# A graph message-passing layer: destination checks moved into the loop over edges, and the order of the last groups changed

## The chip, the cores and the metric

The kernel runs on one core of a Trainium2 chip. A core has a matrix engine (TensorE, PE in the profile; its weight loads are shown apart as PEld), a vector engine (VectorE, DVE), a scalar engine (ScalarE, ACT), GpSimd (POOL) and a sync engine (SP). Each runs its own list of instructions in order and waits on semaphores for the others. DMAs are started by SP, ACT and POOL. The metric is the device time of one execution in microseconds (us); lower is better.

## The reference, cut to what matters

There are N = 6250 nodes of H = 128 features and E = 100000 edges with 4 attributes each. The edges come sorted by destination.

```python
src, dst = edge_index
msg_in = concatenate([x[src], x[dst], edge_features], axis=1)      # E x 260
h = silu(msg_in @ mW1 + mb1)
messages = h @ mW2 + mb2
aggregated = segment_sum(messages, dst, num_segments=N)
u = silu(concatenate([x, aggregated], axis=1) @ uW1 + ub1)
updated = u @ uW2 + ub2
y = layer_norm(x + updated, ln_g, ln_b)
out = layernorm(x + y)                                             # no gain, no bias
```

All is float32.

## The kernel before

**Tables.** msg_in @ mW1 is split by rows of mW1. A table A = x @ mW1[:128] (`tab_a`) and a table B = x @ mW1[128:256] + mb1 (`tab_b`) are made once and stored to DRAM. For an edge, A is gathered by source; B is taken by destination.

**Groups.** The edges are worked on in 98 groups (NG) of 8 tiles of 128 edges (G = 8; the last group, 97, has 6 tiles). Because the edges are sorted, the destinations of one group lie within W = 96 neighbouring nodes from the group's first destination (`base`) on. For a group g:

- `fetch` (L267): POOL starts one indirect DMA per tile, which gathers 128 rows of A into a buffer `ga`. There are six such buffers, so group g+6 waits until group g's buffer has been read. `fetch(g + 4)` is called in iteration g. The first four groups (RAW) gather rows of x instead of A.
- `load` (L536): SP loads 96 rows of B from row `base` on (`mv`) and the edge attributes. The row number is in a register: every 14 groups `load_bases` (L525) reads 14 node numbers from `base_i` into registers of SP and DVE (a TENSOR_LOAD).
- `node_matrix` (L545, DVE) makes a 0/1 matrix `st` of nodes by edges; `edge_matrix` (L557, DVE) a 0/1 matrix `oh` of edges by nodes.
- `products` (L568, PE) adds B's rows and the attributes for each edge into PSUM (`pre`).
- `hidden` (L579): DVE adds gathered A and `pre` into `s` (L587), which frees the gather buffer, and ACT applies silu (L588, `h`). `s` is missing for the first four groups, where PE adds A itself.
- `by_nodes` (L591, PE) sums h over the edges of a node (`pt`, L597), after a transpose of the degree counts (L594). `add` (L600, DVE) adds the sums into the accumulator `acc`, the counts into `deg`.

In iteration g the order is: hidden(g), products(g+2), node_matrix(g+3), edge_matrix(g+1), add(g-2), by_nodes(g). PE, DVE, ACT and SP keep exactly the order in which the Python code calls them (a manual schedule, L111); POOL's only work in the loop is the gathers.

**Nodes.** When all edges of a batch of nodes are done, `node_batch` (L416) does the update for it: two accumulating matmuls and a third for the bias (L455 to L457, `y`), silu (L460, `uT`), a bias row and one matmul per tile (L462, L471), the residual (L473), two layer norms (L473 to L500) and the store (L504). It is a generator: each `yield` ends a step, and the loop runs one step of every running batch per iteration (two in the last six). Batches have 4 tiles of 128 nodes, the last two have 2; the one before the last starts in iteration 96, the last one (`final`) after the loop.

**Start.** Before the loop, POOL gathers for groups 0 to 3, PE transposes x, tables A and then B are made. In between `destination_lists` (L215) makes `rel` (the destination of each edge relative to its group's base), `base_i`, and then a check: the largest and smallest `rel` (L236, L237), 13 memsets (L250) and a few small operations give `bad_i`, which is 1 if some group spans more than 96 nodes or a batch would start too early. At the end every engine reads `bad_i` (L678) and branches to a general path that this data does not take. `fuse_weights` (L405) is called in iteration 5.

The numbers of the lines in this section are those of the kernel before.

Of the kernel before, what the change touches and what calls it, by code (L numbers as in the profile page):

```python
# [24 lines left out]
def kernel(  # L25
# [116 lines left out]
    def by_lane_now(g):  # L142

        t = consts.tile([P, G], I32, name=f"src{g}")
        nc.sync.dma_start(t, src[g * GE : (g + 1) * GE].rearrange("(i p) -> p i", p=P))
        return t

    src_0 = by_lane_now(0)
# [44 lines left out]
    src_i = consts.tile([P, NG, G], I32, name="src_i")  # L193
    rel = consts.tile([P, NG, G], F32, name="rel")
    base_p = consts.tile([P, NG], F32, name="base_p")
    base_i = consts.tile([1, NG], I32, name="base_i")
    bad_i = consts.tile([1, 1], I32, name="bad_i")

# [16 lines left out]
    def destination_lists():  # L215
        base_c = work.tile([NG, 1], F32, name="base_c", bufs=1)
        nc.vector.tensor_copy(base_c, dst_l[:, 0:1])
        rel_n = work.tile([P, GE], F32, name="s")[:NG]
        nc.vector.tensor_scalar(rel_n, dst_l, base_c, None, op0=OP.subtract)

        near_n = work.tile([P, GE], F32, name="s")[:NG]
        nc.vector.tensor_scalar(near_n, rel_n, float(W), -1.0, op0=OP.min, op1=OP.max)
        near_u = tpool.tile([NG, GE], U8, name="near_u")
        nc.vector.tensor_scalar(near_u, near_n, 1.0, None, op0=OP.add)
        nc.sync.dma_start(near_d[:, :], near_u)
        by_lane(rel, rel_n)
        base_f = work.tile([1, NG], F32, name="base_f", bufs=1)
        row = to_row(base_c, NG)
        nc.vector.tensor_copy(base_f, row)
        nc.vector.tensor_copy(base_i, row)  # L230
        p_b = narrow()
        nc.tensor.matmul(p_b[:, :NG], ones[0:1, :], base_f, start=True, stop=True)
        nc.vector.tensor_scalar(base_p, p_b[:, :NG], p_col, None, op0=OP.add)

        far = work.tile([NG, 2], F32, name="far", bufs=1)
        nc.vector.tensor_reduce(far[:, 0:1], rel_n, AX.X, OP.max)  # L236
        nc.vector.tensor_reduce(far[:, 1:2], rel_n, AX.X, OP.min)  # L237
        mid = (W - 1) / 2
        nc.vector.tensor_scalar(far, far, -mid, None, op0=OP.add)
        nc.vector.tensor_mul(far, far, far)  # L240
        nc.vector.tensor_reduce(far[:, 0:1], far, AX.X, OP.max)
        farthest = work.tile([1, 1], F32, name="farthest", bufs=1)
        nc.vector.tensor_reduce(farthest, to_row(far[:, 0:1], NG), AX.X, OP.max)
        bad = work.tile([1, 2], F32, name="bad", bufs=1)
        nc.vector.tensor_scalar(bad[:, 0:1], farthest, mid * mid, None, op0=OP.is_gt)

        below = work.tile([1, NG], F32, name="below", bufs=1)
        nc.vector.memset(below, 0.0)
        for i0, n, g in batches[:-1]:
            nc.vector.memset(below[:, g:], float((i0 + n) * P))  # L250
        nc.vector.tensor_sub(below, below, base_f)
        nc.vector.tensor_reduce(bad[:, 1:2], below, AX.X, OP.max)
        nc.vector.scalar_tensor_tensor(
            bad_i, bad[:, 1:2], 0.0, bad[:, 0:1], op0=OP.is_gt, op1=OP.max
        )
# [66 lines left out]
    def turn_x(i0, n):  # L322
# [2 lines left out]
            nc.tensor.transpose(pt[:, i, :], x_sb[:, i0 + i, :], ident)  # L325
        nc.scalar.copy(xT[:, i0 * P : (i0 + n) * P], pt[:, :n, :].rearrange("p i f -> p (i f)"))

    parts = groups(NT, G)

    def table(i0, n, half):  # L330
# [26 lines left out]
    destination_lists()  # L357
    attribute_rows(0)
    destinations(0)
    for k, (i0, n) in enumerate(parts):  # L360
        if k < RAW:
            turn_rows(k)

        tb = x_sb[:, i0 : i0 + n, :]
        nc.vector.tensor_add(tb, table(i0, n, 1), b1[:, None, :].to_broadcast([P, n, H]))
        nc.sync.dma_start(by_node(tab_b)[:, i0 : i0 + n, :], tb)
# [49 lines left out]
    def node_batch(i0, n, work, new, y, final=False):  # L416
# [30 lines left out]
        if not final:  # L447
# [3 lines left out]
            nc.scalar.copy(flat(deg_b), counts)  # L451
            sums, counts = flat(acc_b), flat(deg_b)
        yield
        y = y()
        nc.tensor.matmul(flat(y), u1x, xT[:, cols], start=True, stop=False)  # L455
        nc.tensor.matmul(flat(y), w2u, sums, start=False, stop=False)  # L456
# [15 lines left out]
        yield  # L472
        nc.vector.tensor_add(y[:, :n], y[:, :n], xs[:, :n])  # L473
        mv = moments(y)
        nc.vector.tensor_add(xs[:, :n], xs[:, :n], b_b[:, None, :].to_broadcast([P, n, H]))
        yield
        r = std(mv)
        yield
# [2 lines left out]
        for i in range(n):  # L481
            nc.vector.scalar_tensor_tensor(  # L482
                y[:, i, :], y[:, i, :], mv[:, i, 0:1], g_b, op0=OP.subtract, op1=OP.mult
            )
            nc.vector.scalar_tensor_tensor(  # L485
                z[:, i, :], y[:, i, :], r[:, i : i + 1], xs[:, i, :], op0=OP.mult, op1=OP.add
            )
        mz = moments(z)
        yield
# [11 lines left out]
                o[:, i, :], z[:, i, :], AF.Identity, bias=shift[:, i : i + 1], scale=rz[:, i : i + 1]  # L501
            )
        yield
        nc.sync.dma_start(rows_of(out), o[:m, :n])  # L504

    def node_tiles(pool, y):
        return pool, lambda name, p=P: pool.tile([p, BT, H], F32, name=name), y
# [14 lines left out]
    nodes = edges.enter_context(tc.tile_pool(name="nodes", bufs=1))  # L522
    stbuf = [held.tile([K1, GE], F32, name=f"st{k}") for k in range(NST)]

    def load_bases(g):  # L525
        _, vals = nc.values_load_multi_w_load_instructions(
            base_i[0:1, g : g + RB],
            engines=(ENG.SP, ENG.DVE),
            min_val=0,
            max_val=NP,  # L530
            skip_runtime_bounds_check_because=IN_RANGE,
        )
        for k, v in enumerate(vals):
            bases[g + k] = v

    def load(g):  # L536

        if g % NQ == 0 and g:
            destinations(g)
        if g % RB == 0:  # L540
            load_bases(g)
        nc.sync.dma_start(mv[g % NM][:W], tab_b[bass.ds(bases[g], W), :])
        nc.sync.dma_start(stbuf[g % NST][W:], ea_d[:, g * GE : (g + 1) * GE])
# [35 lines left out]
    def hidden(g):  # L579
# [8 lines left out]
        nc.scalar.activation(h[:, :n], s[:, :n], AF.Silu)  # L588
        return h

    def by_nodes(g, h, oh):  # L591

        pt = ps.tile([P, 2 * W], F32, name="pt")
        nc.tensor.transpose(pt[0:1, W:], deg_g[:, g : g + 1], ident[:W, :W])  # L594
        n = tiles_of(g)
        for i in range(n):
            nc.tensor.matmul(pt[:, :W], h[:, i, :], oh[:, i, :], start=i == 0, stop=i == n - 1)  # L597
        return pt

    def add(g, pt):  # L600
# [10 lines left out]
    for g in range(NG):  # L611
        if g == 3:
            load_weights()
        if g == 5:
            fuse_weights()
        for c in range(1, NC):
# [14 lines left out]
            node_matrix(g + MADE)  # L631
        if g + 1 < NG:
            oh[g + 1] = edge_matrix(g + 1)
        for k in range(g - 2, g - 1 if not last else g):
            if k in pt:
                add(k, pt.pop(k))
        if not last:
            pt[g] = by_nodes(g, h.pop(g), oh.pop(g))
        for i0, n, first in batches[:-1]:
            if g == first + 1:  # L640
                running.append(node_batch(i0, n, *node_tiles(nodes, node_y)))
        for _ in range(2 if g >= NG - 6 else 1):
            if not last:
                advance(running)

    g = NG - 1
    advance(running)
    before = running[-1]
    next(before)
    pt[g] = by_nodes(g, hidden(g), oh.pop(g))  # L650
    next(before)
    add(g, pt.pop(g))
    final = node_batch(
        *batches[-1][:2],
        nodes,
# [2 lines left out]
        lambda: rows_ps()[:, :BT],  # L658
        final=True,
    )  # L660
    for _ in range(2):
        next(final)
    running = [final, before] + running[:-1]
    while running:
        advance(running)
    edges.close()
# [155 lines left out]
```

## Time and profile before

| | |
|---|---|
| median of 6 runs | 1329.48 us (1324.82 to 1338.0) |
| the profiled execution, its own time | 1321.14 us |
| its span (first to last instruction) | 1319.2 us |
| mean granted TensorE clock | 0.664 of full speed |
| busy: PE / DVE / ACT / POOL | 53% / 36% / 18% / 56% of the span |
| gathers on POOL (L272) | 782, 0.94 us each, started 1.25 us apart at best |

A line of the timeline reads: start, duration, engine, line, operation, result<-operands, shape, count, and in brackets the idle time of that engine before it and what ended it. "issue" is a wait that the profile cannot name, "remote" one whose releaser is not seen. SPq and ACTq are the queues' own instructions: DMA issues and register loads.

### The profile page before, as it was taken

What the parts mean: (1) busy time and instruction counts of PE and PEld (TensorE: products, weight loads), DVE (VectorE), ACT (ScalarE), POOL (GpSimd) and SP (SyncE); (2) the same over time, 40 slices, a digit from 0 to 9 for tenths busy, and PEclk for the clock granted to TensorE, in tenths of its full rate; (3) what the DMA queues carried; (4) which work ended last, traced back from release to release, by engine and by line L of the source; (5) the groups of instructions that cost most, each with busy time, mean ns of one, the idle gap of its engine ahead of it and who ended that gap; (6) DMA issues with size and microseconds to landing.
All of it is one profiled execution on the core that took longest, in us unless ns stands there. A gap on an engine that the chain in (4) does not pass through costs nothing.

```text
span 1319.2 us, 11475 instructions
## 1 busy us (share of the span) xinstructions
PE 705.6 (53%) x3802; PEld 604.5 (46%) x3802; DVE 478.5 (36%) x1018; ACT 239.5 (18%) x293; POOL 739.3 (56%) x790
## 2 busy tenths in 40 slices
PE   3465617347357356456456546465447446345484
PEld 3464516345345344444444544454345345344473
DVE  5143213223423422522522532542423423422563
ACT  1301101210210220211211210310220220210233
POOL 7244565664664664665665665655664664664600
PEclk8677666667666666666666667765767667766685
DMA  6344221221221221222221221221221221221200
GB/s 173 118 120 112 62 58 44 77 68 44 76 72 41 77 77 40 68 61 63 70 75 49 70 70 52 72 68 48 77 75 43 76 75 43 72 70 42 62 16 22
DMA packets 70205, 88.96 MB, mean 67 GB/s; under 512 B 20703, under 2 KB 51822, under 8 KB 70138
## 3 DMA queue, kind: packets, MB, share of 16 engines
q0 software_dynamic: 25024, 51.30, 13.8%
q1 hardware_dynamic: 41578, 35.08, 9.0%
q10 hardware_dynamic: 3536, 1.77, 0.5%
q8 instruction: 32, 0.52, 0.2%
q14 instruction: 35, 0.29, 0.1%
HBM read 76.71 MB, written 11.38 MB: 67 GB/s over the span
## 4 chain that ended last, share of the span: by engine, by line
PE 40%; issue 39%; another core or an unknown queue 6%; DVE 4%; ACT 1%; SPq 0%; DMA 0%; DVEq 0%; ACTq 0%
PE pt L597 17%; PE pre L572 16%; PE y L471 2%; PE y L455 1%; PE y L456 1%; PE y L462 1%; PE y L457 1%; DVE st L547 1%; PE pt L594 1%; DVE oh L560 1%; DVE st L433 0%; DVE z L485 0%; DVE y L482 0%; DVE mv L434 0%
## 5 line engine op out<-in xcount | busy, mean ns | idle before, releaser
L272 POOL DMA_INDIRECT ga<-tab_a,src_i x750 | 707.5, 943 | 500.6 <-DVE s L587 230.5
L597 PE MATMUL pt<-oh,h 128*128 128x96 f32 x1564 | 280.4, 317 | 290.1 <-issue 287.9
L597 PEld LDWEIGHTS pt<-oh,h 128*128 128x128 f32 x1564 | 255.5, 235 | 311.8 <-issue 304.6
L572 PE MATMUL pre<-mv,st 100*128 100x128 f32 x1564 | 283.3, 329 | 181.8 <-issue 171.4
L572 PEld LDWEIGHTS pre<-mv,st 100*128 100x128 f32 x1564 | 252.4, 239 | 208.8 <-issue 207.3
L560 DVE TENSOR_TENSOR oh<-w_row,rel 128x768 f32<-128x768 f32 x98 | 93.1, 950 | 361.0 <-remote 311.9
L587 DVE TENSOR_TENSOR s<-ga,pre 128x1024 f32<-128x1024 f32 x94 | 114.0, 1213 | 279.9 <-issue 193.4
L588 ACT ACTIVATE h<-s 128x1024 f32<-128x1024 f32 x94 | 98.9, 1053 | 610.5 <-DVE s L587 454.3
L547 DVE TENSOR_SCALAR_CACHE_REDUCE st<-near,p_next 96x1024 f32<-96x1024 uint8 x98 | 124.0, 1267 | 4.5 <-DMA ea_d<-pad 3.3
L460 ACT ACTIVATE uT<-y,ub_col 128x512 f32<-128x512 f32 (+2 forms) x13 | 8.4, 646 | 261.9 <-PE y L457 226.8
L473 DVE TENSOR_TENSOR y<-y,xs 128x512 f32<-128x512 f32 (+2 forms) x13 | 8.4, 648 | 109.8 <-issue 104.9
L334 PE MATMUL wide<-w,xT 128*128 128x128 f32 x196 | 32.0, 324 | 18.2 <-issue 10.2
L588 ACT ACT_TABLE_LOAD x25 | 32.1, 1283 | 45.6 <-PE pre L574 43.7
L471 PE MATMUL y<-u,uT 128*128 128x128 f32 x94 | 29.9, 431 | 18.4 <-issue 18.4
L594 PE MATMUL pt<-ident,deg_g 96*1 96x96 f32 x98 | 28.3, 289 | 20.9 <-issue 16.5
L471 PEld LDWEIGHTS y<-u,uT 128*128 128x128 f32 x94 | 24.2, 315 | 32.0 <-issue 32.0
L334 PEld LDWEIGHTS wide<-w,xT 128*128 128x128 f32 x196 | 29.8, 238 | 19.7 <-issue 11.4
L439 ACT ACT_TABLE_LOAD x25 | 32.1, 1283 | 3.9 <-DVE mv L434 3.5
L272 POOL DMA_INDIRECT ga<-in_x_dram,src_i x24 | 23.0, 957 | 7.3 <-issue 7.3
L603 DVE TENSOR_TENSOR acc<-acc,pt 128x96 f32 x98 | 23.6, 241 | 4.4 <-PE pt L597 2.9
L462 PE MATMUL y<-ub_row,ones 1*128 1x512 f32 (+2 forms) x26 | 19.0, 807 | 8.8 <-issue 8.1
L603 DVE TENSOR_TENSOR deg<-deg,pt 1x96 f32 x98 | 22.9, 234 | 0.0
(113 smaller groups left out, 384.2 us busy)
## 6 DMA issues: line engine op xcount, KB each, us to landing
ga<-tab_a,src_i POOLq DMA_INDIRECT x750
near<-near_d SPq DMA_DIRECT2D x24, 384.0 KB
mv<-tab_b SPq DMA_DIRECT2D x98, 48.0 KB
tab_a<-t SPq DMA_DIRECT2D x6, 512.0 KB
tab_b<-x_sb SPq DMA_DIRECT2D x6, 512.0 KB
xs<-in_x_dram SPq DMA_DIRECT2D x11, 256.0 KB
out_dram<-z SPq DMA_DIRECT2D x11, 256.0 KB
st<-ea_d SPq DMA_DIRECT2D x98, 16.0 KB
```

What stands on the lines that cost most here:

```text
L272: nc.gpsimd.indirect_dma_start(out=rows[g][:, i, :], out_offset=None, in_=x if g < RAW else tab_a[:, :], in_offset=bass.IndirectOffsetOnAx ...
L334: nc.tensor.matmul(pm[:, j, :], xT[:, cols], w1[:, half, :], start=True, stop=True)
L462: nc.tensor.matmul(y[:, :n], ones[0:1, :], ub2_row[:, None, :].to_broadcast([1, n, H]), start=True, stop=False,)
L471: nc.tensor.matmul(y[:, i, :], by_p[:, :, i], u2, start=False, stop=i == n - 1)
L547: nc.vector.tensor_scalar(stbuf[g % NST][:W], near.pop(g), p_next, 0.0, op0=OP.is_equal, op1=OP.add, accum_out=deg_g[:, g : g + 1],)
L560: nc.vector.tensor_tensor(oh, w_row[:, None, :].to_broadcast([P, G, W]), rel[:, g, :, None].to_broadcast([P, G, W]), op=OP.is_equal,)
L572: nc.tensor.matmul(pre[:, i, :], st[:, i, :], mv[g % NM], start=True, stop=g >= RAW)
L587: nc.vector.tensor_add(s[:, :n], ga[:, :n], ps[:, :n])
L588: nc.scalar.activation(h[:, :n], s[:, :n], AF.Silu)
L594: nc.tensor.transpose(pt[0:1, W:], deg_g[:, g : g + 1], ident[:W, :W])
L597: nc.tensor.matmul(pt[:, :W], h[:, i, :], oh[:, i, :], start=i == 0, stop=i == n - 1)
L603: nc.vector.tensor_add(at, at, of)
```

## The change

1. `by_lane_now`: the source numbers of group 0 come in two DMAs, column 0 on SP and columns 1 to 7 on ACT (there as the first one), instead of one on SP.
2. The checks of the destinations leave `destination_lists` and become `destination_checks`, called at the top of iteration 4 with a PSUM tile `y`. The largest and smallest `rel` are taken from the transposed tile (128 partitions x 784) instead of the untransposed one (98 x 1024). Two PE instructions go along: the broadcast of the bases (for `base_p`) and the transpose for the maximum.
3. `load_bases(0)` is called ahead of the making of table B instead of behind it.
4. In the iterations 95 and 96 `add(g - 1)` comes directly behind by_nodes(g), and the batch next to last starts in iteration 95.
5. Behind the loop, the rest of the older batches and two steps of the batch next to last come first; then the last group's sum, silu and sums over edges are done in two pieces (4 tiles, then 2), with the step of the first layer norm of the batch next to last between them. A silu of a single element (`primed`) is put ahead of the pieces.
6. In the last batch x + ln_b is made earlier (`xb`), and its result is sent by ACT instead of SP.

```diff
     def by_lane_now(g):
         t = consts.tile([P, G], I32, name=f"src{g}")
-        nc.sync.dma_start(t, src[g * GE : (g + 1) * GE].rearrange("(i p) -> p i", p=P))
+        for eng, lo, hi in ((nc.sync, 0, 1), (nc.scalar, 1, G)):
+            edges = src[g * GE + lo * P : g * GE + hi * P]
+            eng.dma_start(t[:, lo:hi], edges.rearrange("(i p) -> p i", p=P))
         return t
...
         nc.vector.tensor_copy(base_f, row)
         nc.vector.tensor_copy(base_i, row)
-        p_b = narrow()
-        nc.tensor.matmul(p_b[:, :NG], ones[0:1, :], base_f, start=True, stop=True)
-        nc.vector.tensor_scalar(base_p, p_b[:, :NG], p_col, None, op0=OP.add)
-
-        far = work.tile([NG, 2], F32, name="far", bufs=1)
-        nc.vector.tensor_reduce(far[:, 0:1], rel_n, AX.X, OP.max)
-        nc.vector.tensor_reduce(far[:, 1:2], rel_n, AX.X, OP.min)
+
+    def destination_checks(pm):
+
+        nc.tensor.matmul(pm[:, 0, :NG], ones[0:1, :], base_f, start=True, stop=True)
+        nc.vector.tensor_scalar(base_p, pm[:, 0, :NG], p_col, None, op0=OP.add)
+
+        far = work.tile([P, 2], F32, name="far", bufs=1)
+        nc.vector.tensor_reduce(far[:, 0:1], rel, AX.XY, OP.max)
+        nc.vector.tensor_reduce(far[:, 1:2], rel, AX.XY, OP.min)
...
-        nc.vector.tensor_reduce(farthest, to_row(far[:, 0:1], NG), AX.X, OP.max)
+        nc.tensor.transpose(pm[0:1, 1, :], far[:, 0:1], ident)
+        nc.vector.tensor_reduce(farthest, pm[0:1, 1, :], AX.X, OP.max)
...
     destinations(0)
+    load_bases(0)
     for k, (i0, n) in enumerate(parts):
...
         yield
+        xb = xs
+        if final:
+            xb = new("xb")
+            nc.vector.tensor_add(xb[:, :n], xs[:, :n], b_b[:, None, :].to_broadcast([P, n, H]))
         y = y()
...
-        nc.sync.dma_start(rows_of(out), o[:m, :n])
+        (nc.scalar if final else nc.sync).dma_start(rows_of(out), o[:m, :n])
...
-        if g % RB == 0:
+        if g % RB == 0 and g:
             load_bases(g)
...
     for g in range(NG):
         if g == 3:
             load_weights()
+        if g == 4:
+            destination_checks(node_y())
         if g == 5:
             fuse_weights()
...
-        for k in range(g - 2, g - 1 if not last else g):
-            if k in pt:
-                add(k, pt.pop(k))
-        if not last:
-            pt[g] = by_nodes(g, h.pop(g), oh.pop(g))
+        if g - 2 in pt:
+            add(g - 2, pt.pop(g - 2))
+        if last:
+            break
+        pt[g] = by_nodes(g, h.pop(g), oh.pop(g))
+        if g >= NG - 3:
+            add(g - 1, pt.pop(g - 1))
         for i0, n, first in batches[:-1]:
-            if g == first + 1:
+            if g == (first if first >= NG - 3 else first + 1):
                 running.append(node_batch(i0, n, *node_tiles(nodes, node_y)))
...
     g = NG - 1
-    advance(running)
-    before = running[-1]
-    next(before)
-    pt[g] = by_nodes(g, hidden(g), oh.pop(g))
-    next(before)
-    add(g, pt.pop(g))
+    n = tiles_of(g)
+    ga, pg, oh_g, h_g = rows.pop(g), pre.pop(g), oh.pop(g), hbuf[g % NH]
...
+    before = running.pop()
+
+    def piece(lo, hi):
+        nc.vector.tensor_add(s[:, lo:hi], ga[:, lo:hi], pg[:, lo:hi])
+        nc.scalar.activation(h_g[:, lo:hi], s[:, lo:hi], AF.Silu)
+        sums(g, pt[g], h_g, oh_g, lo, hi)
+
     final = node_batch(
...
+    while running:
+        advance(running)
+    for _ in range(2):
+        next(before)
+    next(final)
+
+    nc.scalar.activation(primed, ones[0:1, 0:1], AF.Silu)
+    add(g - 1, pt.pop(g - 1))
+    pt[g] = degrees(g)
+    piece(0, n - 2)
+    next(before)
+    piece(n - 2, n)
+    add(g, pt.pop(g))
     for _ in range(2):
         next(final)
-    running = [final, before] + running[:-1]
+    running = [before, final]
     while running:
         advance(running)
```

`degrees` and `sums` are by_nodes cut in two: the transpose of the counts, and the matmuls of the tiles lo to hi.

## The prediction

> **What bounds the kernel now.** I read the page first (busy times, chain, groups), then the timeline of POOL, PE and DVE at the three places that the change touches: the start, iteration 4 and the end.
>
> ```profile
> PE 705.6 (53%) x3802; PEld 604.5 (46%) x3802; DVE 478.5 (36%) x1018; ACT 239.5 (18%) x293; POOL 739.3 (56%) x790
> PE 40%; issue 39%; another core or an unknown queue 6%; DVE 4%; ACT 1%; SPq 0%; DMA 0%; DVEq 0%; ACTq 0%
> L272 POOL DMA_INDIRECT ga<-tab_a,src_i x750 | 707.5, 943 | 500.6 <-DVE s L587 230.5
> ...
> 64.07 0.32 DVE L233 TENSOR_SCALAR base_p<-wide,p_col 128x98 f32<-128x98 f32 x1 [0.39 <-PE wide L232]
> 64.30 1.21 DVE L236 TENSOR_REDUCE far<-s 98x1 f32<-98x1024 f32 x1
> 70.88 0.15 DVE L253 SCALAR_TENSOR_TENSOR bad_i<-bad 1x1 int32<-1x1 f32 x1
> 71.71 1.22 DVE L342 COPY ga<-wide 128x1024 f32<-128x1024 f32 x1 [0.68 <-DMA ga<-tab_a,src_i]
> 88.88 1.23 DVE L365 TENSOR_TENSOR x_sb<-wide,b 128x1024 f32<-128x1024 f32 x1 [7.25 <-remote]
> 100.10 0.35 DVE L369 MEMSET pad<- 4x352 f32 x1
> 103.74 1.27 DVE L547 TENSOR_SCALAR_CACHE_REDUCE st<-near,p_next 96x1024 f32<-96x1024 uint8 x1 [3.28 <-DMA ea_d<-pad]
> 107.02 0.77 PE L572 MATMUL pre<-mv,st 100*128 100x128 f32 x2 [8.16 <-DMA st<-ea_d]
> ...
> 160.03 1.20 DVE L587 TENSOR_TENSOR s<-ga,pre 128x1024 f32<-128x1024 f32 x1
> 161.50 0.94 POOL L272 DMA_INDIRECT ga<-tab_a,src_i  x1 [5.68 <-DVE s L587]
> 162.95 1.95 PE L597 MATMUL pt<-oh,h 128*128 128x96 f32 x16
> 195.59 0.80 PE L410 MATMUL y<-raw_u1a,w2T 128*128 128x128 f32 x2 [26.90 <-ACT w2T L409]
> 202.20 0.94 POOL L272 DMA_INDIRECT ga<-tab_a,src_i  x1 [11.05 <-DVE s L587]
> ...
> 1290.10 3.73 PE L597 MATMUL pt<-oh,h 128*128 128x96 f32 x16 [1.17 <-ACT h L588]
> 1294.30 0.95 DVE L587 TENSOR_TENSOR s<-ga,pre 128x768 f32<-128x768 f32 x1
> 1302.95 0.47 ACT L460 ACTIVATE ga<-pre,ub_col 128x256 f32<-128x256 f32 x1 [5.32 <-PE pre L457]
> 1307.38 0.41 DVE L473 TENSOR_TENSOR pre<-pre,ga 128x256 f32<-128x256 f32 x1
> 1313.36 0.34 SPq L504 DMA_DIRECT2D out_dram<-ga  x1
> ```
>
> No engine is full. POOL sets the pace: 782 gathers, 1.25 us apart, are 978 us of the 1319, and the 230.5 us behind DVE's `s` are pauses in which POOL waits for a gather buffer. Its timeline is a row of series of 16 or 24 gathers with pauses of 5 to 11 us. About 8 us into a series PE slows from some 9 matmul passes per us to about one in 1 to 2 us, and recovers about 3 us behind the last gather: `L410` waits 26.90 us for a copy whose source was written at 168.42, in a series from 161.50 to 191.5. So a delay of the `s` that starts a series delays POOL, and work that falls early in a series, or in a pause, is quick.
>
> **Part by part, against the profiled 1321.14 us (span 1319.2).** That execution is 8.3 us below the median of 1329.48; I add the sum to both.
>
> *A. Source numbers in two DMAs.* POOL's first gather (4.05) stands 2.52 us for one DMA of 1024 four-byte elements; column 0 is 128 of them. Bounds: at best the whole 2.52 goes; at worst nothing goes and ACT's loads (rows of 0.48 to 0.62 us each) put x_sb 0.6 us later. The first is nearer, since seven eighths of the elements leave SP's queue, but the latency stays: -0.8 (-2.5 to +0.6). The other columns, on ACT from 0.75 on, have until the second gather.
>
> The Trainium skill ("DMA: Bandwidth & Descriptors", "Issuing engines are not separate DMA queues") says that DMAs begun on several engines run on the same 16 DMA engines and that only the sequencer's issue time is saved. By that rule A is worth one issue, 0.45 us by its row, and the sum 0.35 us less; no view of this trace shows the smaller load.
>
> *B. Checks out of the start.* DVE leaves out L233 to L253, from 64.07 to 71.03. In its place stands the register load of C, whose seven DVE rows take 1.31 to 3.79 us, median 3.18: 63.75 + 3.18 + the 0.68 us that the copy at 71.71 waits today = 67.6, so 4.1 us (3.5 to 6) earlier. PE's transposes for it start when the PSUM tile is free, at 63.8 instead of 67.40. Does it reach the end of table B (100.09)? Between 74.7 and 88.9 PE stands in the slow part of the series from 66.27 to 86.2 (the wait of 7.25), which does not move. But work done ahead of it is not left behind it: from 88.9 to 98.65 PE runs 82 passes, 0.12 us each, and 4.1 us of quick time is 34 passes. Both ways give -4.1. Bounds: -1 if the slow part swallows it, -7.6 (64.07 to 71.71) if all counts.
>
> *C. Register load ahead of table B.* SP's row there takes 1.71 us from 102.21 and ends at 103.92, and the load of `mv` follows at 104.35. DVE's own wait ended at 103.74 by the DMA of `pad`, which SP waits for as well. So at most 0.6 goes: -0.5 (-0.6 to 0). On SP the load now stands ahead of the stores of table B, where SP is idle from 70.2 to 75.98.
>
> *D. Checks in iteration 4.* Here is the price. `base_p` waits for a matmul behind by_nodes(3) in PE's order, and behind it on DVE stands s(4) (160.03), which starts the series at 161.50. by_nodes(3) ends at 164.9; with the broadcast (0.46) base_p starts at 165.6, DVE stands 5.5 us. Then 0.25 + two reductions of 784 elements (1.21 x 784/1024 = 0.93 each, 1.8 in sequence) + 0.45 to 168.1, PE's transpose 0.4, then 3.3 us for the maximum, the memsets (2.03) and the end (the rows from 67.65 to 71.03). s(4) runs at 171.9 instead of 160.03, POOL's series starts at 173.4: +11.9. PE waits meanwhile with products(6) until 168.6. What comes back: `fuse_weights` and products(7) then run in the quick part (17 + 5 + 16 passes) instead of the slow one, s(7) comes before the series runs out, and the pause of 11.05 before 202.20 falls away: groups 10 to 13 in one series, group 13 at 203.4, so +1.2 there. After that its pauses stand between other groups, and the distance changes between 0 and one pause (6.5). I take the middle: +3. Bounds: -3 (the moved pauses fall better) to +18.6 (nothing comes back, and one pause of 6.7 more).
>
> The Trainium skill ("TensorE: Matmul & The Clock Gate", Part 1) says that an idle PE falls to half clock and needs about 3.4 us of work to get back; the row at 1290.10 (16 passes 3.73 us after a wait, 1.95 at 162.95) agrees. By it the wait inside D costs another 1.5 us on products(6).
>
> *E. The end.* Up to 1281 nothing changes. By the queues' order and the rows' durations, after: add(94) directly behind add(93) (+0.4), batch 45's first matmuls at 1284.9 (PSUM free at 1284.85) instead of 1293.6, by_nodes(96) 1290.5 to 1294.1. But then L462 and L471 of that batch (1.4) stand ahead of group 97 on PE, and its residual and moments (1.4 us), a memset and add(96) ahead of s(97) on DVE: first piece at 1297.6 against 1294.30, +3.3. The batch's first norm (2.3 us) comes between; second piece to 1300.95, its silu to 1301.5, sums to 1302.2, add, two matmuls, uT at 1305.1 against 1302.95: +2.2. Now the other batch's norm no longer stands ahead of the last residual, which waited from about 1305.9 to 1307.38: 1308.05, +0.7; the addition of b is gone too: the result is sent at 1313.9, +0.5. Then SP today runs its register load (0.65) and some 20 waits of 0.07 us only after that send; ACT has fewer, -1.2. E: -0.7 (-3 to +3; the clock of PE after waits decides).
>
> Sum: -0.8 - 4.1 - 0.5 + 3 - 0.7 = -3.1. Profiled 1318.0, median **1326.4 us**, 0.23% below. A measurement of this kernel can tell about 0.5% (6.6 us) from no change.
>
> **The rivals.**
> - *Faster by over 0.5%.* B reaches its upper bound (-6) and D comes back whole (0 or below). For it: `fuse_weights` loses a 26.90 us wait, and POOL's longest pause early on with it. Against: the pauses recur every 16 to 24 gathers whatever one of them does. -0.8 - 6 - 0.5 - 1.5 - 0.7 = -9.5: 1320.
> - *Slower.* D's delay stays: the series after group 10 is no longer than today's 24, because s(7) is not done before PE slows, and the shifted rhythm meets the batches (one every 8 groups) with one more pause: 11.9 + 6.7 = 18.6, sum +12.5: 1342. It decides from D = 12.7 on (6.6 above no change). For it: s(6) today (171.42) already waited 4.28 in its series. Against: 16 to 24 gathers are no fixed length, and products(6) is done before this series starts.
> - *The start's gain does not arrive*, since the gathers of 66.27 to 86.2 set when PE ends: B = -1, sum 0: 1329.5, within 0.5%.
>
> **How the numbers follow.** As worked out (D between 0 and 6, B near -4): 0.42. Start without gain: 0.08. Faster rival: 0.30. Slower rival: 0.20. The first two lie within 0.5%, so same 0.50, faster 0.30, slower 0.20. The range takes the faster rival to B's end of -7.6 with D at -3 and A at its middle (-13, 1316), and the slower one to a D of 14 or 15 (+9, 1338). The likeliest case alone: 1323 to 1331.
>
> **What would show it.** Right: table B's last addition near 95 instead of 100.09 and the first `pre` near 101.5; DVE idle some 5 us at base_p near 160, then s(4) 12 us behind its add; next a series of 32 gathers, and L410 without its long wait; later series of 16 and 24 as before, from the same groups. At the end s(97) in two pieces with the batch's norm between, and some 4.5 us from the last send to the end instead of 5.8. Wrong: a rhythm other than 24, 24, 16 in the loop (every 8 groups a different time, so tens of us), a table B that still ends at 100, or a PE that slows at iteration 4 outside a series.

## The result: no change that can be measured

| | before | after |
|---|---|---|
| median of all executions | 1330.79 us (78; 1317.83 to 1342.31) | 1331.45 us (36; 1318.19 to 1340.26) |
| ratio to before, 95% interval | | 1.0009 (0.9994 to 1.0025) |
| profiled execution | 1321.14 us | 1326.23 us |
| its span | 1319.2 us | 1324.4 us |

The interval is -0.8 to +3.3 us. Ratios leave out executions that count as disturbed; where few are left their interval is wide and the median of all stands beside it, and in e1, f2, g1 and g2 below the profiled execution is itself such a one, so that for these four the places in the profile say more than the span.

The page of the kernel after: busy times, the chain of work that ended last, and the group of gathers.

```profile
PE 711.8 (54%) x3802; PEld 611.3 (46%) x3802; DVE 477.9 (36%) x1019; ACT 242.7 (18%) x297; POOL 739.2 (56%) x790
issue 42%; PE 40%; DVE 5%; DMA 4%; another core or an unknown queue 1%; ACT 1%; SPq 0%; DVEq 0%; ACTq 0%
L277 POOL DMA_INDIRECT ga<-tab_a,src_i x750 | 707.6, 943 | 505.5 <-DVE s L598 240.5
```

The bound is what it was: POOL 56% busy, and 240.5 us of its idle time behind `s`. What has changed is seen in the timeline of the kernel after, at the start, around iteration 4, and from iteration 95 to the end (columns: start, duration, engine, line, operation, in brackets the idle time before and what ended it).

```profile
3.04 1.11 POOL L277 DMA_INDIRECT ga<-in_x_dram,src  x1 [1.51 <-DMA src<-in_src_dram]
65.85 1.23 DVE L358 COPY ga<-wide 128x1024 f32<-128x1024 f32 x1 [2.65 <-issue]
93.49 1.42 DVE L382 TENSOR_TENSOR x_sb<-wide,b 128x1024 f32<-128x1024 f32 x2 [0.56 <-PE wide L350]
94.93 0.35 DVE L386 MEMSET pad<- 4x352 f32 x1
98.28 0.35 SPq L553 DMA_DIRECT2D mv<-tab_b  x1
101.09 0.77 PE L583 MATMUL pre<-mv,st 100*128 100x128 f32 x2 [7.42 <-DMA st<-ea_d]
106.93 0.94 POOL L277 DMA_INDIRECT ga<-tab_a,src_i  x1 [21.51 <-PE pre L585]
...
158.60 0.32 DVE L237 TENSOR_SCALAR base_p<-y,p_col 128x98 f32<-128x98 f32 x1 [6.23 <-PE y L236]
165.26 1.22 DVE L598 TENSOR_TENSOR s<-ga,pre 128x1024 f32<-128x1024 f32 x1 [0.23 <-issue]
166.59 3.75 PE L583 MATMUL pre<-mv,st 100*128 100x128 f32 x16 [5.00 <-DVE s L598]
166.75 0.94 POOL L277 DMA_INDIRECT ga<-tab_a,src_i  x1 [17.21 <-DVE s L598]
175.61 0.80 PE L427 MATMUL y<-raw_u1a,w2T 128*128 128x128 f32 x2 [1.49 <-issue]
176.85 3.78 PE L583 MATMUL pre<-mv,st 100*128 100x128 f32 x16
200.52 0.33 SPq L553 DMA_DIRECT2D mv<-tab_b  x1
200.58 1.22 DVE L598 TENSOR_TENSOR s<-ga,pre 128x1024 f32<-128x1024 f32 x1 [24.05 <-issue]
200.77 0.37 ACT L481 ACTIVATE uT<-y,ub_col 128x128 f32<-128x128 f32 x1 [17.56 <-remote]
202.07 0.94 POOL L277 DMA_INDIRECT ga<-tab_a,src_i  x1 [5.65 <-DVE s L598]
227.30 0.94 POOL L277 DMA_INDIRECT ga<-tab_a,src_i  x1 [5.55 <-DVE s L598]
...
1282.62 1.22 DVE L598 TENSOR_TENSOR s<-ga,pre 128x1024 f32<-128x1024 f32 x1
1294.13 3.73 PE L609 MATMUL pt<-oh,h 128*128 128x96 f32 x16 [3.71 <-ACT h L599]
1297.78 1.22 PE L483 MATMUL y<-ub_row,ones 1*128 1x256 f32 x2
1300.25 0.43 DVE L494 TENSOR_TENSOR y<-y,xs 128x256 f32<-128x256 f32 x1 [7.34 <-PE y L492]
1302.67 0.67 DVE L676 TENSOR_TENSOR s<-ga,pre 128x512 f32<-128x512 f32 x1
1310.59 0.47 ACT L481 ACTIVATE ga<-pre,ub_col 128x256 f32<-128x256 f32 x1 [4.17 <-PE pre L478]
1313.52 0.43 DVE L494 TENSOR_TENSOR pre<-pre,ga 128x256 f32<-128x256 f32 x1 [0.46 <-PE pre L492]
1319.39 0.60 ACTq L526 DMA_DIRECT2D out_dram<-ga  x1
```

The kernel before at the same places, as far as its lines do not stand above:

```profile
4.05 1.11 POOL L272 DMA_INDIRECT ga<-in_x_dram,src  x1 [2.52 <-DMA src<-in_src_dram]
113.23 0.94 POOL L272 DMA_INDIRECT ga<-tab_a,src_i  x1 [27.29 <-PE pre L574]
228.89 0.94 POOL L272 DMA_INDIRECT ga<-tab_a,src_i  x1 [7.01 <-DVE s L587]
...
1278.95 1.22 DVE L587 TENSOR_TENSOR s<-ga,pre 128x1024 f32<-128x1024 f32 x1
1296.95 0.69 PE L462 MATMUL y<-ub_row,ones 1*128 1x256 f32 x2 [0.56 <-ACT uT L460]
1297.58 0.74 PE L471 MATMUL y<-u,uT 128*128 128x128 f32 x4
```

- **Start.** The first gather stands at 3.04 instead of 4.05, `pad` (behind the last addition of table B) at 94.93 instead of 100.10, the first `pre` at 101.09 instead of 107.02, and the series behind it begins at 106.93 instead of 113.23: 6.3 us earlier.
- **Iteration 4.** Shifted by these 6.3, the next series but one would begin at 155.2 (161.50 before). It begins at 166.75, 11.5 us later than that: DVE stands 6.23 us at `base_p`, then works through the checks, then comes s(4). The second matmul of `fuse_weights` (L427, L410 before) then waits 1.49 us instead of 26.90. The series has 24 gathers as before, and POOL's idle time behind it is 5.65 us instead of 11.05. At gather 121 the kernel after is 1.6 us ahead (227.3 against 228.9): of 11.5 us, 6.9 are back.
- **The rest of the loop**, whose code is the same, takes 1022.6 us before and 1028.0 after from gather 121 to the last. Against the span's difference of 5.2 us this 5.4 looks like the whole story, but it is within chance: in the profiles of the experiments below, the same stretch of nearly the same code takes 1043 to 1067 us, and in the two there that repeat these kernels the sign is the other one (1056.1 before in f4, 1050.1 after in f1).
- **End.** From s(95) on: 41.8 us (1324.4 - 1282.62) instead of 40.3 (1319.2 - 1278.95). s(97) comes 20.0 us behind s(95) instead of 15.3.

So -6.3 at the start, +4.7 in iteration 4, +1.5 at the end: -0.1, with chance in the loop on top.

### The profile page after: what moved, and what is told of

Read it like the earlier page. It is cut to its first block, busy times and chain, and to the rows that moved or that the text cites. A ratio compares the mean times of both kernels' runs of the same rounds, so it can differ in the third digit from the quotient of the medians.

```text
span 1324.4 us, 11483 instructions
## 1 busy us (share of the span) xinstructions
PE 711.8 (54%) x3802; PEld 611.3 (46%) x3802; DVE 477.9 (36%) x1019; ACT 242.7 (18%) x297; POOL 739.2 (56%) x790
## 4 chain that ended last, share of the span: by engine, by line
issue 42%; PE 40%; DVE 5%; DMA 4%; another core or an unknown queue 1%; ACT 1%; SPq 0%; DVEq 0%; ACTq 0%
PE pt L609 16%; PE pre L583 16%; DMA st<-ea_d 3%; PE y L476 1%; PE y L477 1%; PE y L492 1%; PE y L478 1%; DVE s L598 1%; PE pre L585 1%; PE pt L604 1%; PE y L483 1%; DVE st L450 1%; DVE st L558 1%; DVE mv L451 0%
## 5 line engine op out<-in xcount | busy, mean ns | idle before, releaser
L277 POOL DMA_INDIRECT ga<-tab_a,src_i x750 | 707.6, 943 | 505.5 <-DVE s L598 240.5
L609 PEld LDWEIGHTS pt<-oh,h 128*128 128x128 f32 x1564 | 259.5, 238 | 318.1 <-issue 302.6
L583 PE MATMUL pre<-mv,st 100*128 100x128 f32 x1564 | 288.3, 332 | 200.8 <-issue 182.1
L583 PEld LDWEIGHTS pre<-mv,st 100*128 100x128 f32 x1564 | 256.9, 242 | 232.8 <-issue 225.9
L492 PE MATMUL y<-u,uT 128*128 128x128 f32 x94 | 28.5, 430 | 14.6 <-issue 14.4
L492 PEld LDWEIGHTS y<-u,uT 128*128 128x128 f32 x94 | 23.8, 320 | 26.1 <-issue 25.9
L604 PE MATMUL pt<-ident,deg_g 96*1 96x96 f32 x98 | 28.3, 289 | 13.2 <-issue 11.5
L476 PE MATMUL y<-xT,u1x 128*128 128x512 f32 (+2 forms) x26 | 21.9, 944 | 1.2 <-issue 1.1
```

The lines of the kernel that those rows point to most:

```text
L277: nc.gpsimd.indirect_dma_start(out=rows[g][:, i, :], out_offset=None, in_=x if g < RAW else tab_a[:, :], in_offset=bass.IndirectOffsetOnAx ...
L492: nc.tensor.matmul(y[:, i, :], by_p[:, :, i], u2, start=False, stop=i == n - 1)
L583: nc.tensor.matmul(pre[:, i, :], st[:, i, :], mv[g % NM], start=True, stop=g >= RAW)
```

## The experiments

In the experiments the kernel before takes 1355 to 1358 us instead of 1331. They ran on three chips (e on chip 0, f on 3, g on 9); which chip the first result comes from isn't recorded, so the reason is not known. Each is therefore compared with the kernel before beside it, and two are the kernels before and after again. Since chance in the loop is larger than what is asked for, I read three numbers from each profile: the starts of gather 81 (the first behind s(4); "series 5" is the row of gathers that begins with it) and of gather 121, and the time from s(95) to the end. e1, f3, g1 and g2 have 6 executions each, the others 12.

| kernel | gather 81 | gather 121 | between | wait inside fuse_weights | s(95) to end | median (before beside it) | ratio, 95% interval |
|---|---|---|---|---|---|---|---|
| before (first profile) | 161.5 | 228.9 | 67.4 | 26.90 | 40.3 | 1330.79 | |
| after (first profile) | 166.8 | 227.3 | 60.5 | 1.49 | 41.8 | 1331.45 (1330.79) | 1.0009 (0.9994 to 1.0025) |
| f4 before | 164.5 | 232.5 | 68.0 | 26.78 | 40.1 | 1359.01 (1358.38) | 0.9986 (0.9950 to 1.0023) |
| f1 after | 171.6 | 232.6 | 61.0 | 2.23 | 41.5 | 1354.21 (1358.38) | 1.0008 (0.9975 to 1.0041) |
| e2 old end | 172.0 | 232.9 | 60.9 | 1.58 | 40.5 | 1358.03 (1355.95) | 1.0022 (0.9988 to 1.0057) |
| e1 no checks | 160.1 | 227.1 | 67.0 | 26.94 | 41.7 | 1355.70 (1355.95) | 0.9887 (0.9809 to 0.9964) |
| f2 no checks | 160.2 | 228.2 | 68.0 | 27.03 | 41.9 | 1354.88 (1358.38) | 0.9971 (0.9935 to 1.0006) |
| e4 checks at 12 | 157.9 | 226.1 | 68.2 | 27.11 | 41.5 | 1361.49 (1355.95) | 1.0062 (1.0029 to 1.0096) |
| e3 checks behind s(4) | 159.6 | 220.1 | 60.5 | 0.36 | 41.9 | 1343.66 (1355.95) | 0.9946 (0.9907 to 0.9985) |
| g3 checks in three parts | 159.3 | 218.3 | 59.0 | 12.28 | 41.6 | 1344.79 (1355.15) | 0.9931 (0.9892 to 0.9970) |
| f3 three parts, other end | 157.8 | 216.8 | 59.0 | 12.35 | 37.2 | 1338.56 (1358.38) | 0.9858 (0.9818 to 0.9897) |
| g2 the same, fuse_weights at 4 | 159.9 | 219.7 | 59.8 | 3.09 | 37.3 | 1340.90 (1355.15) | 0.9883 (0.9819 to 0.9948) |
| g1 no checks, fuse_weights at 4 | 157.5 | 215.2 | 57.7 | 1.09 | 41.8 | 1351.34 (1355.15) | 0.9877 (0.9783 to 0.9971) |
| g4 before, fuse_weights at 4 | 163.7 | 225.9 | 62.2 | 0.35 | 40.5 | 1349.28 (1355.15) | 0.9990 (0.9948 to 1.0032) |

### What the checks cost: e1 and f2, without them; f1, the kernel after beside them

```diff
+    nc.vector.memset(bad_i, 0)
+    nc.vector.memset(base_p, 0.0)
...
-        if g == 4:
-            destination_checks(node_y())
```

> The kernel after without destination_checks: bad_i and base_p are only set to 0 once, so the test for a group that spans too many nodes is left out. It gives the price of the checks in iteration 4 alone. Theory 1 (the delay of s(4), 11.5 us in the profile after, is paid back only by the pause before the next series, which shrank from 11.05 to 5.65 us; about 6 us stay): 6 us less than the kernel after, 1325 us, ratio to before 0.9955; the series behind the RAW groups starts near 155 instead of 166.75. Theory 2 (my prediction's term D of +3 was right and the missing time was lost elsewhere): 3 us less than after, ratio 0.998. Theory 3 (the rhythm of the gathers absorbs any shift of the start, both ways): no change against after, ratio 1.001.

> The kernel after without destination_checks, again (the test for groups that span too many nodes is left out), since its first measurement had few runs and a wide interval. Theory 1 (about 6 us of the 11.5 us delay of s(4) stay): 6 us less than the kernel after beside it, ratio to before 0.995 to 0.997. Theory 2 (D is +3 as predicted): 3 us less, 0.998. Theory 3 (the rhythm absorbs it): the same as after.

> The kernel after once more, beside the next two, so that they can be compared on one chip. Theory 1 (start -6, checks +6, end +1.4): within 3 us of the kernel before, ratio 0.998 to 1.003, s(95) to the end 41.7 us.

Without the checks series 5 starts at 160.1 (e1) and 160.2 (f2). With them it starts at 172.0 in e2, beside e1 (up to the end, e2 is the kernel after), and at 171.6 in f1, beside f2: the delay is 11.4 to 11.9 us here too. At gather 121 it has shrunk to 5.8 us (227.1 against 232.9) and 4.4 us (228.2 against 232.6). e4 below, which has no checks yet at these places, lies at 157.9 and 226.1, and so 6.8 us ahead of e2 at gather 121. The times don't show it: f2 is 0.9971 and the kernel after beside it 1.0008, 5 us apart with intervals that overlap, and the medians of all executions are 1354.88 and 1354.21; the six executions of e1 say nothing (median 1355.70 beside 1355.95, while their ratio is 0.9887). So theory 3 (all is absorbed) falls by the traces alone, and the 4.4 to 6.8 us seen are nearer to theory 1's 6 than to theory 2's 3.

Series 5 without checks (timeline of f2; L601 is `s`, L430 the second matmul of fuse_weights):

```profile
160.20 0.94 POOL L280 DMA_INDIRECT ga<-tab_a,src_i  x1 [5.81 <-DVE s L601]
167.26 0.27 PE L427 MATMUL y<-ident,raw_w 128*128 128x128 f32 x1
174.49 1.22 DVE L601 TENSOR_TENSOR s<-ga,pre 128x1024 f32<-128x1024 f32 x1 [8.65 <-remote]
194.56 0.80 PE L430 MATMUL y<-raw_u1a,w2T 128*128 128x128 f32 x2 [27.03 <-ACT w2T L429]
201.17 0.94 POOL L280 DMA_INDIRECT ga<-tab_a,src_i  x1 [11.31 <-DVE s L601]
```

fuse_weights begins 7 us into the series, and PE then stands in it until the series of 24 has ended. All else on PE is behind it, and POOL idles 11.31 us afterwards.

### Where the delay stands: e4, the checks at the top of iteration 12

```diff
-        if g == 4:
+        if g == 12:
             destination_checks(node_y())
```

> The kernel after with destination_checks at the top of iteration 12 instead of 4; s(12) starts a series in the steady part of the loop (262.6 in the profile after). Theory 1 (the price is the delay less what the next pause can give back; the pauses there are 6.6 to 7.8 us and the shortest of the loop 5.6, so 1 to 2 us come back of 8 to 11): the 6 us of the start arrive at 220, then +7 to +10; 3 us more than after, ratio 1.003 to 1.004. Theory 2 (such a delay costs 3 us wherever it stands): 3 us less than after, ratio 0.9985.

```profile
267.57 0.32 DVE L237 TENSOR_SCALAR base_p<-y,p_col 128x98 f32<-128x98 f32 x1 [6.05 <-PE y L236]
274.26 1.22 DVE L598 TENSOR_TENSOR s<-ga,pre 128x1024 f32<-128x1024 f32 x1 [0.25 <-issue]
275.75 0.94 POOL L277 DMA_INDIRECT ga<-tab_a,src_i  x1 [19.93 <-DVE s L598]
```

POOL stands 19.93 us (timeline of e4) where it stands about 7 without checks, a delay of 13. At gather 249 this kernel is at 443.5, those with the checks in iteration 4 at 438.4 (e2, beside it) and 436.1 (f1), those without checks at 430.6 and 433.8: 10 to 13 us are still there, and the time is 1.0062 (1.0029 to 1.0096). Theory 1 holds against theory 2, which had 0.9985: the price of a delay is what the pauses behind it don't return. In iteration 4 they return 6 to 7 us, in iteration 12 little or nothing.

### The end: e2, parts 4 to 6 undone

```diff
-        if g >= NG - 3:
-            add(g - 1, pt.pop(g - 1))
...
-            if g == (first if first >= NG - 3 else first + 1):
+            if g == first + 1:
...
+    pt[g] = by_nodes(g, hidden(g), oh.pop(g))
+    next(before)
...
-    piece(0, n - 2)
-    next(before)
-    piece(n - 2, n)
...
-        (nc.scalar if final else nc.sync).dma_start(rows_of(out), o[:m, :n])
+        nc.sync.dma_start(rows_of(out), o[:m, :n])
```

> The kernel after with the end of the kernel before (parts 4, 5 and 6 undone), parts 1 to 3 kept. Theory 1 (the new order of the end costs 1.5 us, as the two profiles show between s(95) and the end: 41.8 us after, 40.3 before): 1.5 us less than after, ratio to before 0.9995, and s(95) to the end again 40.3 us. Theory 2 (the new end is worth -0.7 us as predicted, and the difference in the profiles is chance): +0.7 against after, ratio 1.0015; s(95) to the end between 40 and 42 in a way that does not go with the order.

s(95) to the end is 40.5 us here, 40.1 to 40.5 in the four profiles with the end of before, and 41.5 to 41.9 in the eight with the new one: they don't overlap, and the new end costs 1.4 us. Theory 1 had 1.5. The time itself (1.0022) can't tell so little.

### Behind s(4) instead of ahead of it: e3

```diff
-        if g == 4:
-            destination_checks(node_y())
...
             h[g] = hidden(g)
+        if g == 4:
+            destination_checks(node_y())
```

> The kernel after with destination_checks called behind hidden(4) instead of ahead of it, so that s(4), which starts POOL's series, does not wait for it; s(5) and s(6) do. Theory 1 (what counts is when the series starts, and s(5) need only be done before the first 8 gathers, 10 us, are through): the series starts near 155 instead of 166.75 and runs on; 4 to 6 us less than after, ratio 0.996 to 0.998. Theory 4 (what counts is how much of PE's and DVE's work gets done before PE slows, 8 to 10 us into the series; the checks take 7 us of that away wherever they stand in iteration 4): within 2 us of after, ratio 0.9995 to 1.002, with a longer pause before the next series.

More than any theory had: gather 81 at 159.6, gather 121 at 220.1, 7 to 8 us ahead of the kernels *without* checks (e1 and f2), and 0.9946, if with an interval that reaches theory 1's 0.996 to 0.998. The checks now hold up s(5), and POOL stops after 8 gathers for 4.8 us. In that stop PE is quick again, and fuse_weights, which comes at 176, waits 0.36 us instead of 27.

### The checks in three parts, and another end: f3, g3 and the kernel before, f4

```diff
+        if g == 3:
+            checks_rows(node_y())       # the two PE instructions
...
             h[g] = hidden(g)
+        if g == 4:
+            checks_end()                # base_p, farthest, bad, bad_i on DVE
...
             node_matrix(g + MADE)
+        if g == 2:
+            checks_lists()              # all that needs rel and base_f alone, on DVE
```

and in f3 also

```diff
     while running:
         advance(running)
+    add(g - 1, pt.pop(g - 1))
+    pt[g] = degrees(g)
+    piece(0, n)
+    next(final)
     for _ in range(2):
         next(before)
-    next(final)
     nc.scalar.activation(primed, ones[0:1, 0:1], AF.Silu)
-    add(g - 1, pt.pop(g - 1))
-    pt[g] = degrees(g)
-    piece(0, n - 2)
-    next(before)
-    piece(n - 2, n)
     add(g, pt.pop(g))
-    for _ in range(2):
-        next(final)
-    running = [before, final]
+    next(final)
+    next(before)
+    next(final)
+    running = [final, before]
```

> The kernel after with the checks in three parts (the reductions and memsets on DVE in iteration 2, where DVE stands 20 us before edge_matrix(3); the two PE instructions at the top of iteration 3; the four last DVE instructions, 0.9 us, behind hidden(4)) and with another end: add(96), the whole of s(97), silu and sums come ahead of the residual of the batch next to last, its first norm stands behind add(97), and the last residual is the first to follow. Theory 1 (the checks cost because s(4) waits for them, and the end because s(97) waits 4.7 us longer): series 5 starts as early as without checks, s(95) to the end 37.5 to 38.5 us instead of 41.7, and 9 us less than the kernel after, ratio to before 0.992 to 0.995. Theory 4 (DVE's work counts wherever it stands in the start): 3 to 4 us less than after, from the end alone, ratio 0.998.

> The kernel before itself, for its profile on this chip and for what the comparison gives for no change: ratio 0.998 to 1.002; s(95) to the end 40.3 us; the series behind the RAW groups at 161 us or later.

> The kernel after with the checks in three parts alone; the end as in the kernel after. It separates the two parts of 0.9858. s(95) to the end was 37.2 us there and 41.7 in the kernel after: if the two add up, this one is 4.5 us slower than that one, ratio 0.989 to 0.990, series 5 again 16 gathers and the 121st gather near 217 us (232.6 in the kernel after). If the large gain came from the end or from chance, ratio 0.994 to 0.998 and the 121st gather near 228.

f3 is the fastest of the experiments against the kernel before beside it: 1338.56 us (six executions) beside 1358.38, ratio 0.9858 (0.9818 to 0.9897), where theory 1 had 0.992 to 0.995. Its timeline in iteration 2, in iterations 4 to 7, and at the end:

```profile
110.79 0.96 DVE L238 TENSOR_REDUCE far<-rel 128x1 f32<-128x784 f32 x1
115.74 0.24 DVE L250 TENSOR_REDUCE bad<-below 1x1 f32<-1x98 f32 x1
133.18 0.96 DVE L576 TENSOR_TENSOR oh<-w_row,rel 128x768 f32<-128x768 f32 x1 [17.20 <-PE pt L614]
157.81 0.95 POOL L282 DMA_INDIRECT ga<-tab_a,src_i  x1 [5.91 <-DVE s L603]
180.59 1.22 DVE L603 TENSOR_TENSOR s<-ga,pre 128x1024 f32<-128x1024 f32 x1 [13.66 <-remote]
181.11 0.79 PE L432 MATMUL y<-raw_u1a,w2T 128*128 128x128 f32 x2 [12.35 <-ACT w2T L431]
182.08 0.95 POOL L282 DMA_INDIRECT ga<-tab_a,src_i  x1 [4.57 <-DVE s L603]
...
1298.99 1.22 DVE L603 TENSOR_TENSOR s<-ga,pre 128x1024 f32<-128x1024 f32 x1
1314.70 0.95 DVE L685 TENSOR_TENSOR s<-ga,pre 128x768 f32<-128x768 f32 x1
1316.64 2.88 PE L614 MATMUL pt<-oh,h 128*128 128x96 f32 x12
1324.13 1.22 PE L497 MATMUL pre<-u,ga 128*128 128x128 f32 x4
1325.46 0.43 DVE L499 TENSOR_TENSOR pre<-pre,ga 128x256 f32<-128x256 f32 x1 [2.86 <-PE pre L497]
```

The 5.2 us from 110.79 to 115.98 lie in an idle time of DVE that lasts until 133.18 anyway, so they cost nothing. Series 5 starts as early as without checks and stops after 16 gathers, because s(6) is done only at 180.59 and not at 174.49 as in f2. The second matmul of fuse_weights runs 13 us earlier than in f2 (181.11 against 194.56), and gather 121 starts at 216.8, 10 to 11 us ahead of e1 and f2. At the end s(97) is 15.7 us behind s(95), nearly as before the change (15.3), and the residual waits for nothing but PE: 37.2 us, 2.9 less than before and 4.3 to 4.7 less than after. g3, with the end of the kernel after, has the same start (gather 121 at 218.3) and 41.6 us at the end; its 0.9931 beside 0.9858 is 10 us, where the ends differ by 4.4 and gather 121 by 1.5, with intervals of some 5 us each. It lies between the two outcomes that I had written down, but gather 121 says which: the large gain was there at the start already.

### Is it fuse_weights? g1, g4 and g2, with fuse_weights in iteration 4

```diff
-        if g == 5:
+        if g == 4:
             fuse_weights()
```

> The kernel without destination_checks (the test for groups that span too many nodes is left out), with fuse_weights called in iteration 4 instead of 5. In the profile without checks the first pass of fuse_weights runs 7 us into series 5, its copy on ACT starts only 27 us later, when the series of 24 has ended, and the pause behind is 12.2 us. Theory 5 (the copy inside fuse_weights, stuck in the slow part of the series, is what makes that pause 12 us long and the checks cheap to hide behind): w2T is copied before the series is 6 us old, the pause before the 121st gather's series falls by 4 to 6 us, and the time to 5 us less than without checks, ratio to before 0.990 to 0.993. Theory 6 (the series of 24 itself makes the long pause, whatever stands in it): gathers 105 and 121 start as without checks (201 and 227.7 us), ratio 0.996 to 0.998.

> The kernel before with fuse_weights called in iteration 4 instead of 5, nothing else changed. Theory 5: the 26.90 us wait of its second matmul goes, and with it 4 to 6 us of the pause before gather 105; ratio 0.995 to 0.997. Theory 6: that pause stays at 11 to 12 us; ratio 0.999 to 1.001.

> The kernel with the checks in three parts and the other end (1338.6 us, 0.9858 beside 1358.4), with fuse_weights called in iteration 4, behind the last part of the checks. Its gain was 10 us larger than the sum of its parts, and its series 5 had 16 gathers instead of 24, with a pause of 4.6 us behind it. Theory 5 (fuse_weights was the burden, and the early stop freed it): with fuse_weights out of the slow part the length of series 5 no longer matters; 0.983 to 0.988. Theory 6 (the short series is what gained): if series 5 becomes 24 gathers again, the 10 us are lost, ratio 0.992 to 0.995; if it stays at 16, no change.

```profile
169.02 0.49 PE L410 MATMUL y<-raw_u1a,w2T 128*128 128x128 f32 x2 [0.35 <-issue]
185.05 0.95 POOL L272 DMA_INDIRECT ga<-tab_a,src_i  x1 [1.66 <-issue]
200.43 0.95 POOL L272 DMA_INDIRECT ga<-tab_a,src_i  x1 [5.68 <-DVE s L587]
```

In g4, the kernel before with this one move (timeline), the wait of 26.8 us is 0.35, the pause before gather 105 is 5.68 us where f4 has 11.27, and 5.8 us are gained between gathers 81 and 121; g1 gains 9 to 10 over e1 and f2. g2 gains nothing on top of f3: the two don't add. Read down the column "between": in the five kernels where fuse_weights waits 27 us it is 67.0 to 68.2, in the nine where it waits 12 or less, 57.7 to 62.2. The length of series 5 does not sort them: after, f1 and e2 have 24 gathers and 61 us, e3 has 8 and 60.5, f3 and g3 have 16 and 59. That speaks for theory 5 and against theory 6. In g1 and g2 it isn't a clean separation, since moving fuse_weights shortened series 5 to 16 gathers as well. In g4 POOL stops for only 1.66 us after 16 gathers (185.05) and then goes on to 24, and it is the pause behind that has shrunk, by what theory 5 said. The times settle nothing: g4's median is 1349.28 beside 1355.15, but its ratio of 0.9990 is what theory 6 had and its interval holds both; g1 has 1351.34 beside 1355.15 and a wide interval. A lead at gather 121 need not be a lead in time either: g1 stands there 17 us ahead of f4, the largest lead of all, with a median only 3.8 us below the kernel before beside it. So that the wait inside fuse_weights sets the length of that pause is shown by places in the profiles, one profile for each kernel, and what it is worth in time is not shown. Why s(6) is sometimes held until a series has ended, and sometimes not, stays open.

## Why the prediction was right, and where its steps were not

1326.4 us was forecast, as a sum of -3.1 us; 0.9994 to 1.0025 is -0.8 to +3.3, within 0.5% as the likeliest case had it, and 4 us above its sum. The outcome was right because all terms are small against what can be told from no change, gain and price nearly cancel as it said, and the sum itself lies outside the measured interval: D and E were both too low, by 1.7 and 2.2 us, and the start gave 0.9 more than forecast. Term by term:

- **A, source numbers: -0.8 forecast, -1.0 measured** (first gather 4.05 to 3.04; 3.0 to 3.1 in all experiments that have it, 4.2 and 4.1 in f4 and g4, which don't). The Trainium skill ("DMA: Bandwidth & Descriptors", "Issuing engines are not separate DMA queues") would have given 0.45, the issue alone; here the wait for the load fell from 2.52 to 1.51 us, more than that. What the gather waits for also became an eighth, of which the rule doesn't speak; no run has the smaller load without the second engine.
- **B, checks out of the start: -4.1 forecast; right in its mechanism.** The copy L358 stands at 65.85 instead of 71.71 (-5.9), `pad` 5.2 earlier. Of A's 1.0, 0.5 has arrived at `rel` ahead of it (61.41 instead of 61.88), so B is some 4.7. The copy came 1.8 earlier than worked out (67.6), because DVE stood 2.65 us ahead of it and not 3.18 and 0.68. The rival "the start's gain does not arrive" is out.
- **C, register load: -0.5 forecast, -0.8 measured** (from `pad` to the first `pre` 6.92 before, 6.16 after). The bound of 0.6 was drawn too tight: the load of `mv` came 0.9 nearer to `pad`. The whole start: -5.4 forecast, -6.3 here, and about -5 in the experiments (gather 49 at 115.8 and 115.1 in f4 and g4, 108.9 to 111.7 in the others).
- **D, checks in iteration 4: +3 forecast, +4.7 measured at gather 121** (4.4 to 6.8 in the experiments). The delay was right: 11.9 forecast, 11.5 measured, DVE standing 6.23 us where 5.5 was said. "What comes back" was right in what it named, the wait inside fuse_weights, and wrong in how: the step "s(7) comes before the series runs out ... groups 10 to 13 in one series" failed. s(7) came at 200.58 after 24.05 us of idle DVE, the series had 24 gathers, not 32, and the pause behind it shrank to 5.65 instead of falling away. So 6.9 us came back instead of 8.9. PE's wait was priced too low as well: behind the 5.00 us for s(4) its granted clock is 0.50 from 166.6 to 203 (1.00 from 163.0 to 168.5 in the kernel before), and four blocks of 16 passes up to 186 take 3.62 to 3.78 us, where three such blocks take 1.95 to 1.98 in the kernel before, from 162.95 on; the 1.5 us given with the skill's rule were for the first alone. That doesn't explain s(7): its products end at 180.6 even so, and the last silu before it (ACT, 181.21 to 183.21) ends ahead of the series' last gather (195.48). s(7) starts at 200.58, within 0.3 us of the next instructions of SP (200.52) and ACT (200.77), some 4 us behind that gather. What held them the profile doesn't name, and no run here tells. The slower rival, which needed D at 12.7, was far off in iteration 4; e4 shows it where the checks stand in iteration 12.
- **E, the end: -0.7 forecast, +1.5 measured; this is the one term with the wrong sign** (inside its bounds of -3 and +3). The step that failed is "first piece at ... +3.3": it is +4.7, because L483 and L492 of the batch next to last took 1.22 us each where I had set 0.7 (1.0 of the 1.4 us that it is off), and group 97, the residual of that batch ahead of it on DVE, and the rest came after them. At uT this is +4.0 (forecast +2.2), at the last residual +2.5 (+0.7). Sending by ACT saved 0.8 (5.84 to 5.01 us from the last send to the end; 1.2 forecast). "The clock of PE after waits decides" was the right warning and should have been a number: the row 1290.10 showed 3.73 us for 16 passes behind a wait, and the rows behind it, L455 to L457 at 1.11, 1.06 and 0.87, that it lasts longer than that one row.
- **Loop.** "Later series of 16 and 24 as before, from the same groups" held in the profile of the kernel after, but for one place (between gathers 529 and 568); in the experiments the series differ from profile to profile.

The faster rival asked for B at -6 and D at 0 or below. B went a third of that way, D the other way. That its D can be had is what e3, g3 and f3 show at gather 121 (220.1, 218.3 and 216.8): the delay was needed for nothing, as a later stop of POOL frees fuse_weights there, wholly in e3 (0.36 us) and by half in the others (12.3), and its own move does in g4.

## What to carry to other kernels

A step taken out of the start and put into a paced loop costs the delay of the instruction that restarts the pacing engine, less what the next pauses return; ask which long wait the delay happens to dissolve, and dissolve that one directly. A step with parts on two engines is better cut where the engines change and its parts laid into idle times that are there anyway, with its results read an iteration later. Where the same loop varies by more than the change is worth, compare fixed places (here gather 121, and the time from s(95) on) before spans, and don't take a lead there for one in time (g1).

## What the runs showed of the hardware

- TensorE's clock behind a wait. In all ten profiles that have the matmuls of the batch next to last directly behind by_nodes(96), the new end and that of f3 and g2, PE waits 3.71 us, then takes 3.73 us for 16 passes that take 1.95 elsewhere, and 1.22 us each for L483 and L492 behind them, which take 0.69 and 0.74 in the kernel before; the granted clock is 0.50. In the kernel after PE waits again 6.0 us later. In f3 it works on, from 1310.50 to 1325.35 with one gap of 0.56 us, and the clock stays 0.50 for these 14.9 us, to its last matmul. In the kernel before full speed came 5.4 to 6.9 us after 1290.10 (granted 0.50 up to 1295.5, 0.86 on average from there to 1297.0), and from 1299.8 the clock was 0.50 again, with no wait of PE over 0.56 us between. The Trainium skill ("TensorE: Matmul & The Clock Gate", "Part 1: The HAM clock gate") gives about 3.4 us of sustained work until full clock, and says that the measuring window runs freely and so the number varies. None of these three agrees with 3.4; by it the passes of L483 and L492 would have been 1.0 us shorter, an estimate from that figure and the durations above.
- The same kernel on other chips. The kernel before takes 1330.79 us in the first result and 1355 to 1358 on the chips 0, 3 and 9, at a mean granted clock of 0.664 in the first profile and 0.655 in f4; the pauses behind gather 121 sum to 197 us in the first profile of it and 229 in f4, with gathers at the same 1.25 us.
